# GRU gates by seven block products instead of eight, with partial sums forked in PSUM, in a four-layer graph network on one core

## The chip, the cores and the metric

The kernel runs on one core of a Trainium2 chip. The metric is device time in microseconds, as the median of the runs; the profile is of one further execution. PE is TensorE, PEld its weight load, DVE VectorE, ACT ScalarE, POOL GpSimd, SP the engine whose queue issues most of the DMAs. All matrices are float32.

## The reference

128 graphs of 128 nodes with 256 features go through four layers, each followed by a residual addition and a layernorm: `x = layernorm(x + layer(x, adj))`.

- Layer 0 is graph attention with 4 heads (scores, leaky relu, masked softmax, weighted sum, elu).
- Layer 1 is a gated graph network: three rounds of message passing, each with a GRU cell with shared gate weights.
- Layer 2 is a relational sum: one masked neighbour sum and one weight for each relation number in `adj`.
- Layer 3 is graph attention with one head.

The change is mostly about layer 1:

```python
for i in range(3):
    m = einsum("bnd,de->bne", h, weight[i])
    aggr = einsum("bst,bsd->btd", A, m)
    gi = aggr @ w_ih.T + b_ih            # i_r, i_z, i_n
    gh = h @ w_hh.T + b_hh               # h_r, h_z, h_n
    r = sigmoid(i_r + h_r)
    z = sigmoid(i_z + h_z)
    n = tanh(i_n + r * h_n)
    h = (1 - z) * n + z * h
```

## The kernel before, in words

**Tiles and stages.** The graphs are cut into 33 groups: 31 of four graphs, and a half group of two at each end. A tile of a full group has 128 partitions and 4 x 128 = 512 columns for each half of the features (`C = 2` halves). A group passes through `loads`, `head` (layer 0, L387), `body` (layer 1, L486) and `tail` (layers 2 and 3, L622). Each of these is a Python generator that records a few instructions at a time and yields.

**What sets the order.** Three strings of letters (`START`, `STEPS`, `END`, L42 to L61) say which generator takes the next step; a letter stands for a stage and a group relative to the current one (L43 to L54, L782 to L788). Each engine then runs its instructions in exactly the order in which they were recorded. In the middle, one pass through `STEPS` handles a head of a later group, the bodies of two groups and tails of earlier ones; such a pass is called a period here. Semaphores make an engine wait for another one's data or for a buffer to come free.

**Gates.** `fold` (L234) multiplies `weight[l]` into `w_ih` once, so that a round needs only the neighbour sum of h, called `agT`, and a folded weight `wc`. A gate (r, z, and the two parts of n, called nh and ni) is then a sum over h (`whh`) and `agT` (`wc`). For each output half c, `part` (L519) issues one matmul of 128 x 128 weights by 512 columns per input half and source into a bank of PSUM; `gate` has four banks and the other uses (`ps`) have four. So r and z take 8 matmuls a round each and nh and ni take 4 each. A float32 matmul of the program becomes two weight loads and two matmul instructions in the profile, so the profile's counts are twice the program's.

**The rest of a round.** ACT applies tanh to r and z (`sigmoid`, L535) and reads nh with its bias (L541); DVE combines r and nh (L543) and adds ni (L547); ACT takes tanh (L549); POOL forms h - n (L551); DVE finishes h (L557, L558). PE transposes h (L104), ACT copies it to SBUF (L509), PE multiplies by the adjacency, and DVE copies the result to `agT` (`neighbours`, L475 to L483).

**Other places.** `head` adds the attention score's row part, column part and mask in one DVE instruction per head and graph (L426), as `tail` does (L731); leaky relu and the row maximum follow on DVE (`softmax_unscaled`, L347 to L350), exp on ACT (L353). elu's minimum is on DVE (L332). Transposes that PE doesn't do go through DRAM: `to_dram` (L255) writes a tile, `from_dram` (L265) reads it back in four DMAs that permute 32 x 32 squares into one of four buffers `sq`, and DVE transposes inside the squares into another tile (L289, L391, L454, L648, L664, L751). `layernorm` (L293) writes its result to a new tile. All these DMAs are on SP's queue.

The instructions after the main part, which redo the work for relation numbers above 1, do not run with these inputs.

Of the kernel before, what the change touches and what calls it, by code (L numbers as in the profile page):

```python
# [16 lines left out]
P = 128  # L17
# [8 lines left out]
GATES, OTHERS = 4, 4  # L26
# [10 lines left out]
TERMS = {"r": {"h0", "h1", "a0", "a1"}, "z": {"h0", "h1", "a0", "a1"}, "nh": {"h0", "h1"}, "ni": {"a0", "a1"}}  # L37
# [3 lines left out]
FIRST = {"a": ("c", 0), "b": ("f", 0), "c": ("l", 0), "d": ("h", 0), "e": ("l", 1), "f": ("h", 1), "g": ("l", 2), "h": ("b", 0), "i": ("h", 2)}  # L41
START = """  # L42
abcbaaccabadbdaadddddddddaabeeacddadabbbbbbbbbbddbddbbdbbbbbbfbbbbbbbbdddddddddddgddddbbddddddfbbfdd  # L43
dddddffffdbfffffffdfddddfdgfhdfffehfbhhhfffffhhhhhhhhhhhhhfhhfhhhhhhfihhhhhhhfhhhhhhhhffhhhhhiffhhhh
hhhhhhfhhfhfhhhhhhhffffhihhhhhiffbiffhihffhbfiihfiihihhhihhh
"""
PERIOD = {"a": ("t", -2), "b": ("h", 0), "c": ("l", 2), "d": ("b", -1), "e": ("h", 1), "f": ("b", 0), "g": ("t", -3), "h": ("h", 2), "i": ("t", -1), "j": ("l", 1), "k": ("l", 0)}
STEPS = """
abbcaaaadadaeaddddddeabdddddeeeeafadbdfbegbcffddeeeeaaeeddddddfefaddfffaffffffffffffeffffffefhffiaff
aiiiefafffffaaffieiiafaifiiififaiaaaijfiifafaafafffiffiieffiiiikefffiaiifefaefffafiafefafffeefffehff  # L50
ffhfieeeeeefhhffhfhheieiehhfeefhh
"""
LAST = {"a": ("t", -3), "b": ("b", -2), "c": ("h", -1), "d": ("t", -4), "e": ("b", -1), "f": ("t", -2), "g": ("t", -1), "h": ("l", -1)}
END = """  # L54
aaaabbacbaacbbbcaabbbbbbbbbbdbccaabbbbabbbaeacebeeaafeeeeaeeefeeeeeeeeeeeeeeeeeeeefeaeeeeeeefafeffff
fffaaeaeefffafeaaaaafffffeeeffafefeefeeeeaaeffeeeeeeeeaeeeeeeeeeeeeeeeeeefefafeeefffeffeffeefeeeefgg
effffaeeeeeeefeeeeeeehffgggggggfagggggfggggggfgggfggffgfffggggfgfffggggggggagggfggfgggfgffgfgggggggg
ggggggggg
# [8 lines left out]
def kernel(ctx: ExitStack, tc: tile.TileContext, a: dict, out: bass.AP):  # L67
# [20 lines left out]
    def bank(*shape, tag="ps"):  # L88

        t = ring(pp, [P, 512], F32, tag, tag, GATES if tag == "gate" else OTHERS)  # L90
        n = 1
        for s in shape:
            n *= s
        if len(shape) == 1:
            return t[:, :n]
        names = "abcd"[: len(shape)]
        sizes = {k: s for k, s in zip(names[1:], shape[1:])}
        return t[:, :n].rearrange(f"p ({' '.join(names)}) -> p {' '.join(names)}", **sizes)
# [26 lines left out]
    def load_adj(st):  # L125
        st["adj"] = ring(sp, [P, st["n"], N], I32, "adj", f"adj_{st['g']}", 5)
        nc.sync.dma_start(st["adj"], adj[st["graphs"]].rearrange("g n m -> n g m"))

# [13 lines left out]
    def loads(st):  # L142
        for load in (load_x_squares, load_adj, load_rows, load_adj_squares):
            if st["g"] != 0 or load is load_adj_squares:
                load(st)
            yield

    def state(g):
        by_pe = {"head": g == 0, "tail": g == NG - 1}
        return {"g": g, "graphs": spans[g], "n": sizes[g], "relations": 1, "by_pe": by_pe}  # L150
# [10 lines left out]
    vec = ring(sp, [P, 4, D], F32, "y", "vec", 2)  # L161
# [5 lines left out]
    for l, tag in enumerate(("hr", "xb", "x3T")):  # L167
        w1.append(sp.tile([P, C, D], F32, tag=tag, name=f"w1_{l}"))
        nc.scalar.dma_start(w1[l], a["L1_gnn_weight"][l].rearrange("(c p) o -> p c o", p=P))
        if l == 0:  # L170
            for e, tag in enumerate(("wh3", "x2_0")):
                wih.append(sp.tile([P, 3 * D], F32, tag=tag, name=f"wih_{e}"))
                nc.scalar.dma_start(wih[e], a["L1_gnn_w_ih"][e * P : (e + 1) * P, :])
    whh = cp.tile([P, C, 3 * D], F32, tag="whh", name="whh")
    nc.scalar.dma_start(whh, a["L1_gnn_w_hh"].rearrange("(c p) o -> p c o", p=P))
# [23 lines left out]
    wc = cp.tile([P, L, C, 3 * D], F32, tag="wc", name="wc")  # L199
# [33 lines left out]

    def fold(st):  # L234


        for l in range(L):
# [8 lines left out]
            for c in range(C):  # L246
                for lo, hi in ((0, 512), (512, 3 * D)):
# [4 lines left out]
                    nc.vector.tensor_copy(wc[:, l, c, lo:hi], ps)  # L252
                    yield

# [10 lines left out]
    def from_dram(name, d):  # L265

        t = ring(sp, [P, d.shape[0]], F32, "sq", f"sq_{name}", 4)
# [3 lines left out]
    def turn_rows(st, x, tag, name, by_pe):  # L271

        n = x.shape[1]
        if by_pe:
            yield
            yield
            t = sp.tile([P, C, n * N], F32, tag=tag, name=name)
# [5 lines left out]
        else:  # L283
            d = to_dram(name, *(x[:, :, ts(c, P)] for c in range(C)))
            yield
            s = from_dram(name, d)
            yield
            t = sp.tile([P, C, n * N], F32, tag=tag, name=name)
            nc.vector.transpose(t.rearrange("p c m -> p (c m)"), s)  # L289
# [3 lines left out]
    def layernorm(y, st, name, bufs=1):  # L293
# [11 lines left out]
        def rest():  # L305
# [7 lines left out]
            o = st[name] = ring(sp, [P, n, D], F32, name, f"{name}_{g0}", bufs)  # L313
            for g in range(G):
                if g < n:
                    nc.scalar.activation(  # L316
                        o[:, g, :], y[:, g, :], AF.Identity, bias=mr[:, g : g + 1], scale=rs[:, g : g + 1]
# [6 lines left out]
    def residual_elu_norm(y, xin, st, name, layer, bufs=1):  # L324

        g0 = st["g"]
        half, rest = layernorm(y, st, name, bufs)
        ts_ = {}
        for k in range(0, G, 2):
            if k < st["n"]:  # L330
                t = ts_[k] = ring(sp, [P, 2, D], F32, "elu", f"elu_{layer}_{g0}_{k}", 2)
                nc.vector.tensor_scalar(t, y[:, k : k + 2], 0.0, None, ALU.min)  # L332
# [12 lines left out]
        yield from rest()  # L345

# [40 lines left out]
    def head(st):  # L387

        g0, n, adj_t, by_pe = st["g"], st["n"], st["adj"], st["by_pe"]["head"]
        xT = sp.tile([P, C, n * N], F32, tag="x0T", name=f"x0T_{g0}")  # L390
        nc.vector.transpose(xT.rearrange("p c m -> p (c m)"), st["x0s"].rearrange("p c m -> p (c m)"))  # L391
# [3 lines left out]
        if st["relations"] < R:  # L395
            above = sp.tile([P, n, N], F32, tag="adj_T", name=f"above_{g0}")
# [17 lines left out]
        for k in range(0, G, 2):  # L414
            if k >= n:
                for _ in range(8):
                    yield
                continue
            em = ring(sp, [P, 2, H, N], F32, "em", f"em0_{g0}_{k}", 2)
            for g in range(k, k + 2):  # L420
# [4 lines left out]
                for h in range(H):  # L425
                    nc.vector.scalar_tensor_tensor(  # L426
# [434 lines left out]
```

## Time and profile before

| what | value |
| --- | --- |
| median of 3 runs | 2969.25 us (2967.49 to 2970.28) |
| the profiled execution: device time | 2971.45 us |
| the profiled execution: span, first to last instruction | 2969.7 us |
| TensorE clock granted | 0.993 |
| busy: PE, DVE, ACT, POOL | 2898.6, 2026.4, 1326.1, 564.7 us |
| DMA | 254.93 MB, q1 busy 41.9% of 16 engines |
| one period of the middle, 1398.50 to 1488.85 us | 90.35 us |

How to read it: the lines that carry the prediction are quoted in it. The page gives the busy time of each engine, the chain of work that ended last (which engine and tile the end was waiting for at each moment, as shares of the span), and groups of equal instructions with count, busy time and mean length of one. The mean length of a matmul counts time that overlaps its neighbours, so the distance between starts in the timeline tells how long it occupies PE. In a timeline row, square brackets give the idle time of the engine just before, and what ended it. Busy shares are averages over the whole span.

### The profile page before, as it was taken

The numbers are of one execution on the slowest core, as the hardware profiler recorded it, in microseconds if no ns is written. First come the engines' busy times: TensorE is split into PE (matmuls) and PEld (weight loads), VectorE is DVE, ScalarE is ACT, GpSimd is POOL, SyncE is SP. The second block draws the span as 40 slices with busy tenths as digits, with TensorE's granted clock in tenths as the row PEclk, the third lists the DMA queues.
The fourth block names the chain that finished last, engine by engine and source line by source line (L and its number), as shares of the span: only waits on it lengthen the run. The fifth ranks groups of instructions, "written<-read, shape, count | busy, mean of one in ns | idle before, by whom it ended". The sixth has DMA issues, their size and how long they took to land.

```text
span 2969.7 us, 34231 instructions
## 1 busy us (share of the span) xinstructions
PE 2898.6 (98%) x10918; PEld 1691.9 (57%) x10918; DVE 2026.4 (68%) x4456; ACT 1326.1 (45%) x3310; POOL 564.7 (19%) x529
## 2 busy tenths in 40 slices
PE   7999999999999999999999999999999999999995
PEld 5655555555555555555555555555555555555564
DVE  5666767666767666767666677667676667676565
ACT  3444444444444444444444444444444444444343
POOL 0111222211222211222111222111222112222121
PEclk9999999999999999999999999999999999999997
DMA  4434444444445444445444444434444434444321
GB/s 112 80 79 80 89 86 92 85 98 84 85 82 100 85 96 84 80 84 102 88 89 83 88 82 97 95 77 91 93 82 93 97 78 89 86 88 84 75 54 42
DMA packets 1160922, 254.93 MB, mean 86 GB/s; under 512 B 931488, under 2 KB 1160224, under 8 KB 1160736
## 3 DMA queue, kind: packets, MB, share of 16 engines
q1 hardware_dynamic: 1157536, 248.87, 41.9%
q10 hardware_dynamic: 3200, 3.81, 0.5%
q8 instruction: 88, 1.44, 0.2%
q14 instruction: 98, 0.80, 0.1%
HBM read 144.97 MB, written 107.61 MB: 85 GB/s over the span
## 4 chain that ended last, share of the span: by engine, by line
PE 92%; DVE 4%; issue 1%; ACT 1%; DMA 1%; POOL 0%; DVEq 0%; SPq 0%; ACTq 0%; POOLq 0%
PE gate L101 63%; PE ps L101 27%; PE ps L104 2%; DVE d L557 2%; DVE aT L751 1%; ACT z L535 1%; PE psb L375 0%; DMA wih<-in_L_gnn_w_ih_dram 0%; DMA x<-in_x_dram 0%; ACT em L353 0%; DVE em L349 0%; DMA d_h0T<-x 0%; ACT x L316 0%; DVE st_x L303 0%; DMA vec<-in_L_gnn_a_src_dram 0%
## 5 line engine op out<-in xcount | busy, mean ns | idle before, releaser
L101 PE MATMUL gate<-agT,wc 128*128 128x512 f32 (+1 forms) x2376 | 1116.3, 583 | 3.3 <-DVE agT L483 3.3
L101 PEld LDWEIGHTS gate<-agT,wc 128*128 128x128 f32 x2376 | 444.1, 190 | 478.0 <-issue 459.4
L101 PE MATMUL gate<-h2T,whh 128*128 128x512 f32 (+1 forms) x792 | 375.9, 584 | 0.0
L101 PE MATMUL gate<-h1T,whh 128*128 128x512 f32 (+1 forms) x792 | 373.7, 581 | 0.0
L101 PE MATMUL gate<-h0T,whh 128*128 128x512 f32 (+1 forms) x792 | 362.5, 580 | 1.3 <-DVE h0T L289 1.3
L557 DVE SCALAR_TENSOR_TENSOR d<-z,d 128x512 f32<-128x512 f32 (+1 forms) x198 | 159.8, 807 | 270.9 <-ACT z L535 227.3
L543 DVE SCALAR_TENSOR_TENSOR n<-r,n 128x512 f32<-128x512 f32 (+1 forms) x198 | 132.9, 671 | 265.4 <-ACT n L541 265.3
L353 ACT ACTIVATE em<-em,nm 128x128 f32<-128x128 f32 x640 | 247.9, 391 | 52.9 <-DVE nm L350 52.9
L535 ACT ACTIVATE z<-gate,bhalf 128x512 f32<-128x512 f32 (+1 forms) x198 | 132.7, 670 | 257.0 <-PE gate L101 256.9
L316 ACT ACTIVATE x<-y,mr_x,rs_x 128x256 f32<-128x256 f32 x384 | 199.5, 591 | 100.2 <-DVE mr_x L311 100.2
L101 PEld LDWEIGHTS gate<-h0T,whh 128*128 128x128 f32 x792 | 145.4, 191 | 150.6 <-issue 149.3
L551 POOL TENSOR_TENSOR d<-h2T,n 128x512 f32<-128x512 f32 (+1 forms) x66 | 82.8, 1255 | 751.7 <-ACT n L549 751.7
L309 POOL TENSOR_TENSOR rs_x<-rs_x,neghalf 128x4 f32<-128x4 f32 (+1 forms) x99 | 108.4, 1095 | 612.3 <-DVE rs_x L308 612.2
L101 PEld LDWEIGHTS ps<-wh,aT 128*128 128x128 f32 x1280 | 171.5, 192 | 90.6 <-issue 49.2
L549 ACT ACTIVATE n<-n,bih 128x512 f32<-128x512 f32 (+1 forms) x198 | 139.6, 705 | 174.4 <-DVE n L547 172.9
L101 PEld LDWEIGHTS gate<-h2T,whh 128*128 128x128 f32 x792 | 146.0, 191 | 125.2 <-issue 113.4
L535 ACT ACTIVATE r<-gate,bhalf 128x512 f32<-128x512 f32 (+1 forms) x198 | 132.3, 668 | 190.2 <-PE gate L101 190.1
L101 PE MATMUL ps<-wh,aT 128*128 128x64 f32 (+1 forms) x1280 | 191.8, 297 | 17.9 <-DVE aT L751 13.5
L483 DVE COPY agT<-ps 128x512 f32<-128x512 f32 (+1 forms) x198 | 129.0, 652 | 113.2 <-PE ps L101 113.2
L101 PEld LDWEIGHTS gate<-h1T,whh 128*128 128x128 f32 x792 | 143.6, 191 | 109.9 <-issue 105.2
L541 ACT ACTIVATE n<-gate,bhn 128x512 f32<-128x512 f32 (+1 forms) x198 | 133.2, 673 | 146.7 <-PE gate L101 146.7
L551 POOL TENSOR_TENSOR d<-h0T,n 128x512 f32<-128x512 f32 (+1 forms) x66 | 82.1, 1244 | 528.0 <-ACT n L549 528.0
(116 smaller groups left out, 4030.7 us busy)
## 6 DMA issues: line engine op xcount, KB each, us to landing
d_em<-em SPq DMA_DIRECT2D x63, 512.0 KB, 3.4
sq_em<-d_em SPq DMA_DIRECT2D x252, 128.0 KB, 3.9
x0s<-in_x_dram SPq DMA_DIRECT2D x248, 64.0 KB, 2.7
x<-in_x_dram SPq DMA_DIRECT2D x31, 512.0 KB, 5.5
d_h0T<-x SPq DMA_DIRECT2D x62, 256.0 KB, 2.5
sq_h0T<-d_h0T SPq DMA_DIRECT2D x124, 128.0 KB, 3.2
d_h<-h3T SPq DMA_DIRECT2D x62, 256.0 KB, 2.4
sq_h<-d_h SPq DMA_DIRECT2D x124, 128.0 KB, 3.2
```

The lines of the kernel that those rows point to most:

```text
L101: nc.tensor.matmul(ps, lhsT, rhs, start=start, stop=stop)
L104: nc.tensor.transpose(ps, src, ident)
L309: nc.gpsimd.tensor_tensor(rs, rs, neghalf[:, :n], ALU.pow)
L316: nc.scalar.activation(o[:, g, :], y[:, g, :], AF.Identity, bias=mr[:, g : g + 1], scale=rs[:, g : g + 1])
L353: nc.scalar.activation(em[:, r, :], em[:, r, :], AF.Exp, bias=nm[:, i : i + 1], accum_out=den[:, i : i + 1])
L483: nc.vector.tensor_copy(into[c], ps.rearrange("p g n -> p (g n)"))
L535: nc.scalar.activation(t, gate[name][0], AF.Tanh, bias=bhalf[:, col : col + 1], scale=0.5)
L541: nc.scalar.activation(n, gate["nh"][0], AF.Identity, bias=bhn[:, c : c + 1], scale=0.5)
L543: nc.vector.scalar_tensor_tensor(n, tr, 1.0, n, ALU.add, ALU.mult)
L549: nc.scalar.activation(n, n, AF.Tanh, bias=bih[:, 2 * C + c : 2 * C + c + 1])
L551: nc.gpsimd.tensor_sub(d, hT[:, c, :], n)
L557: nc.vector.scalar_tensor_tensor(d, tz, 1.0, d, ALU.add, ALU.mult)
```

## The change

- **Gates.** The 2 x 2 block product (output halves by input halves, with the 512 columns cut into two halves of 256) is done by seven products of 128 x 128 by 256 columns in place of eight, in Winograd's form of Strassen's scheme. The left-hand sums of weights are formed once (`left_factors`); the right-hand sums of h and of `agT` are formed by POOL, four subtractions each per round and group (`right_sums`). A gate holds two PSUM banks, `sums` (output half 0) and `gate` (output half 1), two of each kind. Products 1 and 5 land in PSUM; ACT copies product 1 to the other bank and product 5 to SBUF; the later products accumulate on these copies; DVE adds product 5 to an intermediate sum twice.
- **Lanes.** `body` is replaced by four generators: `reset_and_new` (r, then ni), `new_and_update` (nh, then z), and one for each output half (`chunk_0`, `chunk_1`) with the elementwise steps. The three strings are new, and name these lanes.
- **Transposes in place.** The squares are loaded into the tile in which DVE then transposes them, source and destination the same; the buffers `sq` are gone. `layernorm` also writes over its input, and several tiles share or lose buffers. `adj` is loaded a second time for layer 3.
- **Moved between engines.** `agT` is copied by ACT (was DVE). The score is formed by an ACT addition of row and column part (`plus`, one per head and graph) and a POOL addition of the mask (was one DVE instruction). elu's minimum is on POOL (was DVE). Layer 2's bias is added by POOL to x2 in place, a little later.

The diff, cut to its core:

```diff
-GATES, OTHERS = 4, 4
+GATES, OTHERS = 2, 4
-TERMS = {"r": {"h0", "h1", "a0", "a1"}, "z": {"h0", "h1", "a0", "a1"}, "nh": {"h0", "h1"}, "ni": {"a0", "a1"}}
+TERMS = {"r": "ha", "z": "ha", "nh": "h", "ni": "a"}
...
+    def left_factors(l):
+        f = [factors[l][:, :, k] for k in range(S)]
+        nc.vector.tensor_add(f[4], f[6], f[3])
+        nc.vector.tensor_sub(f[5], f[4], f[0])
+        nc.vector.tensor_sub(f[2], f[1], f[5])
+        nc.vector.tensor_sub(f[6], f[0], f[6])
...
-        t = ring(sp, [P, d.shape[0]], F32, "sq", f"sq_{name}", 4)
         squares(t, d)
...
-            t = sp.tile([P, C, n * N], F32, tag=tag, name=name)
-            nc.vector.transpose(t.rearrange("p c m -> p (c m)"), s)
+            t = ring(sp, [P, C, n * N], F32, tag, name, bufs)
+            flat = from_dram(t.rearrange("p c m -> p (c m)"), d)
+            yield
+            nc.vector.transpose(flat, flat)
...
-                nc.vector.tensor_scalar(t, y[:, k : k + 2], 0.0, None, ALU.min)
+                nc.gpsimd.tensor_scalar(t, y[:, k : k + 2], 0.0, None, ALU.min)
...
+    def plus(e, row, col):
+        nc.scalar.activation(e, row, AF.Identity, bias=col)
...
-                    nc.vector.scalar_tensor_tensor(
-                        em[:, g - k, h, :], ps[:, h, :], wh[:, g, D + h : D + h + 1], nbias[:, g, :], ALU.add, ALU.add
-                    )
+                    plus(em[:, g - k, h, :], ps[:, h, :], wh[:, g, D + h : D + h + 1])
+                yield
+                e = em[:, g - k]
+                nc.gpsimd.tensor_add(e, e, nbias[:, g, :].unsqueeze(1).to_broadcast([P, H, N]))
...
+    def right_sums(t, B, c, name):
+        half = t.shape[1] // 2
+        lo, hi = t[:, :half], t[:, half:]
+        def minus(k, x, y):
+            B[k] = ring(sp, [P, half], F32, "T", f"T{k}_{name}", 12)
+            nc.gpsimd.tensor_sub(B[k], x, y)
+        if c == 0:
+            minus(5, hi, lo)
+        else:
+            minus(6, hi, B[5])
+            yield
+            minus(7, hi, B["12"])
+            minus(4, lo, B[6])
+        yield
...
-        nc.vector.tensor_copy(into[c], ps.rearrange("p g n -> p (g n)"))
+        nc.scalar.copy(t, ps.rearrange("p g n -> p (g n)"))
...
+    def gates(st, names):
+        cols = st["n"] * N
+        half = cols // 2
+        for l, layer in enumerate(st["layers"]):
+            for name in names:
+                first, second = bank(cols, tag="sums"), bank(cols, tag="gate")
+                layer["gates"][name] = first, second
+                c11, c12, c21, c22 = first[:, :half], first[:, half:], second[:, :half], second[:, half:]
+                def product(into, k, source, start=False, name=name, l=l, layer=layer):
+                    w = factors["h" if source == "h" else l]
+                    nc.tensor.matmul(
+                        into, w[:, SEL[name], k - 1], layer[source][k], start=start, stop=True, skip_group_check=True
+                    )
+                for i, source in enumerate(TERMS[name]):
+                    product(c21, 1, source, start=i == 0)
+                    yield
+                    product(c22, 5, source)
+                    yield
+                nc.scalar.copy(c11, c21)
+                p5 = ring(sp, [P, half], F32, "p5", f"p5_{name}{l}_{st['g']}", 3)
+                nc.scalar.copy(p5, c22)
+                yield
+                for source in TERMS[name]:
+                    product(c11, 2, source)
+                    yield
+                for source in TERMS[name]:
+                    product(c21, 6, source)
+                    yield
+                nc.vector.tensor_add(c12, c21, p5)
+                yield
+                for source in TERMS[name]:
+                    product(c12, 3, source)
+                yield
+                for source in TERMS[name]:
+                    product(c21, 7, source)
+                yield
+                nc.vector.tensor_add(c22, c21, p5)
+                yield
+                for source in TERMS[name]:
+                    product(c21, 4, source)
+                yield
```

## The prediction

> **What bounds the kernel now.** I read the page's busy times first, then its chain of work that ended last, then a stretch of the middle.
>
> ```profile
> span 2969.7 us, 34231 instructions
> PE 2898.6 (98%) x10918; PEld 1691.9 (57%) x10918; DVE 2026.4 (68%) x4456; ACT 1326.1 (45%) x3310; POOL 564.7 (19%) x529
> PE 92%; DVE 4%; issue 1%; ACT 1%; DMA 1%; POOL 0%; DVEq 0%; SPq 0%; ACTq 0%; POOLq 0%
> PE gate L101 63%; PE ps L101 27%; PE ps L104 2%; DVE d L557 2%; DVE aT L751 1%; ACT z L535 1%; PE psb L375 0%; DMA wih<-in_L_gnn_w_ih_dram 0%; DMA x<-in_x_dram 0%; ACT em L353 0%; DVE em L349 0%; DMA d_h0T<-x 0%; ACT x L316 0%; DVE st_x L303 0%; DMA vec<-in_L_gnn_a_src_dram 0%
> 1398.50:1488.85 90.35, 89.85 (x340) 51.98 (x340) 63.26 (x139) 41.45 (x103) 17.56 (x16) 1.00 0.43 88
> ```
>
> TensorE is the path: 92% of the chain, 63% in the gate products. The last line is one period of the middle (one group of four graphs): of 90.35 us TensorE is busy 89.85, VectorE 63, ScalarE 41, GpSimd 18. So a microsecond taken from TensorE counts in full while the others keep up.
>
> What a matmul occupies is read from starts in the timeline, not from its mean, because matmuls overlap (columns: start, length, form, count):
>
> ```profile
> 1477.00 1.95 PE L101 MATMUL ps<-rel,x 128*128 128x128 f32 x16
> 1478.79 1.88 PE L101 MATMUL gate<-agT,wc 128*128 128x512 f32 x4
> 1480.51 3.62 PE L101 MATMUL ps<-w,hr 128*128 128x256 f32 x16
> 1483.96 1.02 PE L101 MATMUL gate<-agT,wc 128*128 128x512 f32 x2
> ```
>
> 512 columns: (1480.51-1478.79)/4 = 0.430 us. 256 columns: (1483.96-1480.51)/16 = 0.216. 128 columns: (1478.79-1477.00)/16 = 0.112. A float32 matmul of the program is two such instructions. So the 256-column matmul, with a fresh weight each, already runs at half the price of the 512-column one; this matters below.
>
> The one place in the period where TensorE waits:
>
> ```profile
> 1465.11 2.49 POOL L651 TENSOR_TENSOR y<-y,x 128x512 f32<-128x512 f32 x2 [0.77 <-DVE y L648]
> 1466.51 1.64 DVE L557 SCALAR_TENSOR_TENSOR d<-z,d 128x512 f32<-128x512 f32 x1 [1.55 <-ACT z L535]
> 1468.18 0.69 DVE L558 SCALAR_TENSOR_TENSOR h1T<-d,n 128x512 f32<-128x512 f32 x1
> 1468.79 0.71 DVE L751 STREAM_TRANSPOSE aT<-sq_em 128x512 f32<-128x512 f32 x1
> 1469.55 1.13 PE L101 MATMUL ps<-wh,aT 128*128 128x256 f32 x4 [0.50 <-DVE aT L751]
> ```
>
> L557 takes 1.64 us in place of 0.69 while GpSimd adds at L651, everything behind it in VectorE's queue is late, and TensorE loses 0.50 us. The groups by form show the same block, in the 512-column row of L349, slower than the 1024-column one:
>
> ```profile
> L349 DVE SCALAR_TENSOR_TENSOR em<-em 128x1024 f32<-128x1024 f32 x64 | 77.8, 1216 | 0.0
> L349 DVE SCALAR_TENSOR_TENSOR em<-em 128x512 f32<-128x512 f32 x31 | 50.4, 1626 | 0.1
> L551 POOL TENSOR_TENSOR d<-h2T,n 128x512 f32<-128x512 f32 x62 | 80.0, 1290 | 718.9 <-ACT n L549 718.9
> L547 DVE TENSOR_TENSOR n<-n,gate 128x256 f32<-128x256 f32 x12 | 5.0, 416 | 2.1 <-PE gate L101 1.2
> ```
>
> **What the Trainium skill says.** "SBUF — State Buffer", section "Who interferes with whom": VectorE's second read port is GpSimd's, and one instruction holds it to its end; a VectorE instruction with two SBUF inputs collides, one with a PSUM input does not. The trace agrees (1.626 against 0.69 us above). "TensorE: Matmul & The Clock Gate", section "LDWEIGHTS": a weight load takes its columns over 1.2 GHz, 107 ns for 128; records here show 190 ns, and the 0.112 us spacing fits 107. "ScalarE: Activation LUTs", section "What ACT_TABLE_LOAD costs": an ACTIVATE with one pointer operand takes 280 + 0.833 N ns, about 93 of which overlap its neighbour; for N = 128 an estimate of 0.29 to 0.39 us; no row here is that exact form.
>
> **The change, part by part.**
>
> *Gate products.* There are 6 pairs (r, z from h and a; n from h; n from a) x 3 layers x 31 full groups = 558. Each goes from 4 matmuls of 512 columns to 7 of 256: 4 x 2 x 0.430 = 3.44 us becomes 7 x 2 x 0.216 = 3.02, less 0.42; over 558, -232 us (between -228 and -234 by the rounding). The 36 pairs of the two half groups: 4 x 2 x 0.216 against 7 x 2 x 0.112, 0.16 less each, -6. All on the path: -234 us taken together with the rounding, giving 2736.
>
> *VectorE.* Removed: the score adds (640, 140 + 36 us), the agT copies (129), elu's minimum (65). Added: two PSUM adds per gate, 744 of 256 columns at 0.416 (L547's row) = 310, and 14 for the half groups. Net -46: 1980 us, 72% of 2736.
>
> *ScalarE.* Added: two forks per gate, 744 copies of 256 columns at 0.37 (copies of that width from PSUM: 363 to 374 ns) = 275; the score add, 640 at 0.29 to 0.39, taken 0.30 = 192; agT copies 186 x 0.58 = 108. 1326 becomes 1900, 69%.
>
> *GpSimd.* Added: right-hand sums, 744 of 256 columns at 0.77 (the L551 rows of that width: 724 to 824) = 571, 24 for half groups; score additions of 512 columns, 159 x 1.27 = 202; elu's minimum 128 x 0.8 (between 0.5 and 1.27) = 102. 565 becomes 1464, 54%.
>
> No engine but TensorE is full, so none of this is on the path by its sum. What is on the path is the handoffs.
>
> *New waits.* Each gate now has three of them, 12 gates a group: products 1 and 5, then ScalarE forks, then product 2; product 6, then a VectorE add, then products 3 and 7; product 7, another add, then product 4. TensorE runs in order, so a late fork or add stops everything behind it, the other gate, heads and tails included. I laid the changed program's TensorE order against the rows above: between producer and consumer stands, at the median, 1.02 us of other matmuls for a fork that needs 0.49 (0.37 + two signals of 0.06), and 0.86 us for an add that needs 0.53. So about half of the handoffs have under 0.5 us to spare, where the waits of before mostly had 1 to 5 us. One has less than nothing: with two gate banks in place of four, "ni" reuses r's bank, and its first product stands 0.43 us behind r's last, while ScalarE's read needs 0.80: 0.37 x 93 = +34 us.
>
> *The shared port.* Before, blocking costs VectorE 26 us (L557: 186 x 0.14), 29 (L349) and 16 (L332), 71 in all; L332 moves away, 55 remain. GpSimd's work grows 2.6-fold: 55 x 2.6 = 143 us. From above: some 1030 two-input VectorE instructions meet GpSimd busy 54% of the time, 0.45 us left: 250. Before, TensorE lost 0.5 of 2.3 us blocked per period. With under half the slack I take half of 143: +72; ends 0 and 250.
>
> *Squares transposed in place.* Same transposes, same sizes: nothing, bounds -10 to +10 (an in-place form isn't in the trace). The load into its own square now waits on SP for the square's last reader, and SP's later loads queue behind it; these readers are 20 us or more past in the written order at the median, which hides it; uncovered, it would be a 3 us landing per group, +90. Reloading adj: 33 DMAs, 8 MB on 255, DMA at 43%: nothing. In-place layernorm, later xb, other tags: same counts. The prologue gains 16 VectorE additions of 384 columns at about 0.55 and a four-part load: +8, from 0 to +15, uncovered because TensorE idles there already.
>
> *Sum against the profiled execution:* 2969.7 - 234 + 34 + 72 + 8 = 2850. Its device time is 2971.45, 1.75 more than the span; the median of the runs, 2969.25, is 2.2 below that. They cancel: 2850.
>
> **The rivals.** (1) *The handoffs stay covered*, as the period of before shows a written order can: 2736 + 34 = 2770. For it: medians above need. Against: FIFO queues at 70% and an unplanned port block. (2) *Port and queues jam*, gain mostly lost: the port would carry GpSimd's 1464 and about 730 of VectorE, 80% of 2736. With 200 of the 250 on TensorE: 2736 + 34 + 170 to 200 = 2940 to 2970; I take 2940. (3) *Slower*: the adds, in VectorE's queue behind blocked two-input work, expose time at each handoff. Place: the PSUM adds before products 3, 7 and 4, and the forks; 36 a group, 1116 in all. The gain is gone at 234/1116 = 0.21 us each; at 0.3 it is 335 - 234: 3070. For it: spare time of 0.33 us at the median add, and L557's block of 0.95. Against: one late handoff gives slack to the next. (4) *It does not do what it says*: the 256-column products run at 0.245 us or more, since each needs its weights in that time, and the 234 vanish: 3000 with the waits. The 0.216 row speaks against it.
>
> **How the numbers follow.** Forecast 0.55 (own range 2800 to 2915), (1) 0.15, (2) 0.15, (3) 0.12, (4) 0.03. A fifth of (2) ends within 0.2% of before, 6 us, about what a measurement of this kernel can tell from no change: same 0.03. Faster 0.55 + 0.15 + 0.12 = 0.82, slower 0.15. The range 2755 to 2970 leaves out (3), (4) and the low edge of (1).
>
> **What would show it.** Right: gate matmuls at 0.216, a period of 85 to 88 us with TensorE idle 3 to 6 us of it, idle put down to the sums and gate tiles; L557-like rows with means over 0.8. Gate intervals near 0.245 show (4); a period of 84 shows (1); VectorE idle before TensorE's waits would refute the port as cause. I am wrong if TensorE's largest waits are on DMA or ScalarE.

## The result, and the profile after

The changed kernel takes 3017.5 us (median of 4 runs, 3012.9 to 3022.3) against 2968.4 for the kernel before (4 runs, 2967.3 to 2970.3): 1.0165 times as long, interval [1.0147, 1.0183]. The forecast was 2850, with a range up to 2970.

The page of the kernel after; the lines answer to those shown of before (span, busy times, chain by engine, chain by line):

```profile
span 3016.8 us, 44962 instructions
PE 2802.2 (93%) x14486; PEld 2310.3 (77%) x14486; DVE 2186.4 (72%) x4298; ACT 1830.2 (61%) x4952; POOL 1658.1 (55%) x1610
PE 69%; DVE 12%; POOL 8%; ACT 5%; issue 4%; DMA 1%; SPq 1%; POOLq 0%; DVEq 0%; ACTq 0%
PE gate L586 36%; PE ps L115 16%; PE sums L586 16%; POOL x L741 3%; DVE d L658 2%; POOL d L653 2%; ACT r L638 2%; DVE mr_x L357 1%; DVE h1T L659 1%; POOL em L794 1%; DVE h3T L659 1%; ACT em L394 1%; PE ps L118 1%; ACT x L362 1%; DVE o L387 1%
```

TensorE's share of the chain has fallen from 92% to 69%; VectorE and GpSimd took most of the rest, though they are busy only 72% and 55% of the time. One period of the middle (view of busy times by stretch):

```profile
1406.70:1497.98 91.28, 86.48 (x443) 71.37 (x443) 67.52 (x131) 56.57 (x153) 51.76 (x49) 0.98 0.47 91
```

It lasts 91.28 us. TensorE is idle for 4.8 of them (0.5 before), and the granted clock, the third number from the end, is 0.98 in place of 1.00. The period of before is 89.70 us, from the start of one transposition of h (1398.55) to the next (1488.25); the stretch of 90.35 us in the table above is a little longer than a period. After, periods of 91.28 and 89.65 us alternate in most of the middle, where 85 to 88 was forecast; over 27 periods the mean is 90.70. So of the time that the kernel lost, these 27 periods hold some 27 us, and what lies outside them, the start and the end of the program, some 20. What TensorE waited for, from the view of the waits (total us, times, longest):

```profile
PEld L424 <- DVE split L420: 84.7, 33, 3.5
...
PEld gate L586 <- POOL T_a L550: 54.1, 90, 1.2
PEld gate L586 <- ACT r L638: 42.1, 67, 0.8
...
PEld gate L586 <- DVE gate L614: 34.2, 73, 0.6
```

The largest is one wait per period, at an instruction that the diff does not touch: the transposition (L424) of the attention scores that VectorE splits into three bf16 parts. Its place, from the timeline over all engines (start, length, idle time before it in brackets):

```profile
1464.94 1.27 POOL L794 TENSOR_TENSOR em<-em,nbias 128x512 f32<-128x512 f32 x1 [4.00 <-ACT em L394]
1466.30 1.78 POOL L653 TENSOR_TENSOR d<-h2T,n 128x512 f32<-128x512 f32 x1
...
1468.11 1.20 DVE L658 SCALAR_TENSOR_TENSOR d<-z,d 128x512 f32<-128x512 f32 x1 [0.45 <-POOL d L653]
...
1468.85 1.05 POOL L550 TENSOR_TENSOR T_h<-h0T,T_h 128x256 f32<-128x256 f32 x1
...
1469.35 1.10 DVE L659 SCALAR_TENSOR_TENSOR h3T<-d,n 128x512 f32<-128x512 f32 x1
...
1469.86 1.17 POOL L550 TENSOR_TENSOR T_a<-agT 128x256 f32<-128x256 f32 x1
1470.37 0.69 DVE L417 CAST split<-wh 128x16 bf16<-128x16 f32 x1
1471.00 0.72 POOL L550 TENSOR_TENSOR T_h<-h0T 128x256 f32<-128x256 f32 x1
1471.10 0.65 DVE L418 TENSOR_TENSOR rest<-wh,split 128x16 f32<-128x16 f32 x1
...
1471.68 0.72 POOL L550 TENSOR_TENSOR T_h<-h0T,T_h 128x256 f32<-128x256 f32 x1
1471.78 0.65 DVE L419 CAST split<-rest 128x16 bf16<-128x16 f32 x1
...
1472.69 0.24 PE L424 MATMUL psb<-identb,split 128*48 128x128 bf16 x1 [2.24 <-DVE split L420]
```

Read it from the bottom. TensorE waits 2.24 us for the split. The split is four instructions of 16 columns; three of them take 0.65 to 0.69 us (the fourth 0.18, with no sum beside it); each ends with a GpSimd right-hand sum (T). They stand in VectorE's queue behind d and h3T, which the sums have stretched as well (1.20 and 1.10 in place of 0.69), and d waited for GpSimd's subtraction, behind GpSimd's new mask sum.

TensorE's waits can be added up without the modelled ends of matmuls: the distance from each matmul's start to the next, less the undisturbed spacing (0.430, 0.216 or 0.112 us for 512, 256 or 128 columns), summed over the span. Before: 112.6 us. After: 385.2. So the matmuls themselves gave back (2969.7 - 112.6) - (3016.8 - 385.2) = 225 us, and 273 were lost over that spacing: in waits, and in stretches at half the clock, which are found below. The experiments ask which part of the change these 273 belong to.

### The profile page after: what moved, and what is told of

It reads as the page before. It is cut to its first block, busy times and chain, and to the rows that moved or that the text cites. A ratio compares the mean times of both kernels' runs of the same rounds, so it can differ in the third digit from the quotient of the medians.

```text
span 3016.8 us, 44962 instructions
## 1 busy us (share of the span) xinstructions
PE 2802.2 (93%) x14486; PEld 2310.3 (77%) x14486; DVE 2186.4 (72%) x4298; ACT 1830.2 (61%) x4952; POOL 1658.1 (55%) x1610
## 4 chain that ended last, share of the span: by engine, by line
PE 69%; DVE 12%; POOL 8%; ACT 5%; issue 4%; DMA 1%; SPq 1%; POOLq 0%; DVEq 0%; ACTq 0%
PE gate L586 36%; PE ps L115 16%; PE sums L586 16%; POOL x L741 3%; DVE d L658 2%; POOL d L653 2%; ACT r L638 2%; DVE mr_x L357 1%; DVE h1T L659 1%; POOL em L794 1%; DVE h3T L659 1%; ACT em L394 1%; PE ps L118 1%; ACT x L362 1%; DVE o L387 1%
## 5 line engine op out<-in xcount | busy, mean ns | idle before, releaser
L586 PE MATMUL gate<-T_a,factors 128*128 128x256 f32 (+1 forms) x2376 | 708.2, 385 | 21.8 <-POOL T_a L550 21.6
L586 PE MATMUL gate<-T_h,factors_h 128*128 128x256 f32 (+1 forms) x2376 | 701.9, 382 | 10.1 <-DVE gate L614 3.8
L586 PEld LDWEIGHTS gate<-T_a,factors 128*128 128x128 f32 x2376 | 433.7, 192 | 110.9 <-POOL T_a L550 54.1
L586 PEld LDWEIGHTS gate<-T_h,factors_h 128*128 128x128 f32 x2376 | 441.0, 193 | 94.6 <-DVE gate L614 34.2
L586 PE MATMUL sums<-agT,factors 128*128 128x256 f32 (+1 forms) x1188 | 347.7, 384 | 0.6 <-ACT sums L596 0.4
L362 ACT ACTIVATE x<-x,mr_x,rs_x 128x256 f32<-128x256 f32 x384 | 199.6, 589 | 157.3 <-DVE mr_x L357 157.2
L586 PEld LDWEIGHTS sums<-agT,factors 128*128 128x128 f32 x1188 | 224.4, 194 | 40.2 <-DVE sums L606 8.6
L479 POOL TENSOR_TENSOR em<-em,nbias 128x512 f32<-128x512 f32 x128 | 179.8, 1415 | 39.3 <-ACT em L394 38.3
L394 ACT ACTIVATE em<-ps,wh 128x128 f32<-128x128 f32 x640 | 185.2, 387 | 20.9 <-PE ps L115 18.1
L586 PE MATMUL gate<-agT,factors 128*128 128x256 f32 (+1 forms) x594 | 180.4, 385 | 16.3 <-ACT r L638 12.9
```

The lines of the kernel that those rows point to most:

```text
L362: nc.scalar.activation(y[:, g, :], y[:, g, :], AF.Identity, bias=mr[:, g : g + 1], scale=rs[:, g : g + 1])
L394: nc.scalar.activation(e, row, AF.Identity, bias=col)
L479: nc.gpsimd.tensor_add(e, e, nbias[:, g, :].unsqueeze(1).to_broadcast([P, H, N]))
L586: nc.tensor.matmul(into, w[:, SEL[name], k - 1], layer[source][k], start=start, stop=True, skip_group_check=True)
```

## The experiments

Theory A: GpSimd's added work, in its queue and on the port that it shares with VectorE, makes releases late. Theory B: the handoffs within a gate (fork, two PSUM adds) cost by themselves, which was rival 3. Times are medians of 4 runs (of 20 for e10); the kernel before, measured alongside, took 2966.5 to 2968.3.

### The two suspects, alone and together

**e1.** The sums are left out:

```diff
-            nc.gpsimd.tensor_sub(B[k], x, y)
+            B[k] = x
```

> The right-hand sums are left out (products 4 to 7 read a block of h or agT itself), so GpSimd loses 798 subtractions, some 600 us; the 7 products, the forks and the two adds stay. Theory A (GpSimd's added work makes the releases late, by its own queue and by the shared port): TensorE's waits fall by more than half, 2840 to 2890 us. Theory B (the three handoffs per gate cost by themselves, about 0.2 us each): only the waits on the sums go, 2950 to 2980 us.

2858.8 us, 0.964 [0.9624, 0.9657] of before. The 798 subtractions cost 159 us. The rows of one split instruction, after and then without the sums (busy us, mean ns):

```profile
L417 DVE CAST split<-wh 128x16 bf16<-128x16 f32 x31 | 20.9, 673 | 0.0
```

```profile
L417 DVE CAST split<-wh 128x16 bf16<-128x16 f32 x31 | 5.2, 167 | 0.0
```

and TensorE's wait for the split without the sums, 84.7 us in the kernel after:

```profile
PEld L424 <- DVE split L420: 14.9, 31, 2.7
```

**e2.** The handoffs are left out:

```diff
-                nc.scalar.copy(c11, c21)
-                nc.scalar.copy(p5, c22)
...
-                    product(c11, 2, source)
+                    product(c11, 2, source, start=i == 0)
...
-                nc.vector.tensor_add(c12, c21, p5)
...
-                nc.vector.tensor_add(c22, c21, p5)
```

> The forks (two ScalarE copies a gate) and the two VectorE adds a gate are left out; the 7 products and the right-hand sums stay, so partial sums are not combined. Theory A: GpSimd is as busy as in the changed kernel, only some waits go, 2950 to 2990 us. Theory B: the handoffs were the loss, 2780 to 2840 us.

3016.5 us, no change. VectorE is busy 279 us less, and it gains nothing.

**e7.** Both edits together.

```diff
-            nc.gpsimd.tensor_sub(B[k], x, y)
+            B[k] = x
...
-                nc.vector.tensor_add(c12, c21, p5)
```

> Both the right-hand sums and the forks and adds are left out; the 7 products stay. With GpSimd relieved, do the handoffs cost anything? If they do: 2790 to 2825 us, well under the 2859 without the sums alone. If they are hidden: 2845 to 2860 us.

2828.3 us, 30.5 below e1: without the sums the handoffs do cost 30. Why they seemed free in e2 is seen in the clock. Granted clock by stretch in the kernel after, around the wait of 2.24 us, which ends at 1472.69 (the third number from the end):

```profile
1468.00:1472.60 4.60, 2.45 (x15) 1.88 (x13) 4.35 (x6) 2.00 (x9) 4.32 (x6) 1.00 0.29 88
1472.60:1474.60 2.00, 1.91 (x13) 1.27 (x13) 0.04 (x1) 1.26 (x4) 0.00 (x0) 0.92 0.64 131
1474.60:1476.00 1.40, 1.40 (x4) 1.17 (x4) 0.00 (x0) 1.40 (x7) 1.14 (x2) 0.50 1.00 157
1476.00:1478.00 2.00, 2.00 (x7) 1.60 (x6) 0.00 (x0) 2.00 (x8) 2.00 (x3) 0.58 1.14 153
1478.00:1480.00 2.00, 2.00 (x11) 1.69 (x10) 0.94 (x3) 0.36 (x2) 1.45 (x2) 1.00 0.52 70
```

From 1.6 us after the end of the wait TensorE runs at half its clock, for 3.4 us; in the middle of the span this happens in every second period. 256-column matmuls with a spacing of 0.38 to 0.46 us count it: 131 in the kernel after, 12 in e1, 272 in e2, where nearly every period has it. At 0.216 each, e2 loses 30 us more to the clock than the kernel after. Summed over all matmuls in the stretches that the trace's clock records give as half clock, the time over the undisturbed spacing is 71 us in e2, 36 in the kernel after and 9 in e1, which makes it 35. That is about what e2's missing handoffs gained: "no change" was two effects of nearly the same size, as far as these sums tell.

### What of the sums costs: their time, their reads, or the dependence

**e5.** The sums on VectorE.

```diff
-            nc.gpsimd.tensor_sub(B[k], x, y)
+            nc.vector.tensor_sub(B[k], x, y)
```

> The right-hand sums are formed by VectorE in place of GpSimd, all else as in the changed kernel. GpSimd loses some 600 us, VectorE gains 798 instructions at about 0.42 us, 320 us in all, and would stand near 2300 us of a span of 2900. Theory A (GpSimd's queue and port): most of what leaving the sums out gave comes back although the work is done, 2880 to 2930 us. If the dependence itself (h or agT, then four subtractions, then the product) made the loss, whoever does it: 3000 us or more.

3016.9 us, no change, with VectorE busy 2311 us: the sums are then late in VectorE's queue (products of T_a stand 106 us over the spacing, 64 in the kernel after).

**e9.** Each sum on 32 of its 256 columns.

```diff
-            nc.gpsimd.tensor_sub(B[k], x, y)
+            nc.gpsimd.tensor_sub(B[k][:, :32], x[:, :32], y[:, :32])
```

> Each right-hand subtraction is done on 32 of its 256 columns (the rest of its tile keeps zeros), by GpSimd, in the same place of its queue and with the same waits for h or agT and of TensorE for it. GpSimd loses some 400 us. If the time that GpSimd's sums take (its queue, the port) is the cause: 2870 to 2910 us, near the 2859 with no sums. If it is the dependence, an additional engine in the chain from h to the product: 2970 us or more.

2862.3 us, 3.5 above e1. The instructions, their places in the queue and what they wait for are all there, at 0.25 to 0.49 us each on average. So the dependence costs next to nothing; the time of each sum is the cost.

**e10.** GpSimd is kept busy as long, but reads nothing.

```diff
-            nc.gpsimd.tensor_sub(B[k], x, y)
+            for _ in range(3):
+                nc.gpsimd.memset(B[k], 0.5)
```

> Each subtraction is replaced by three memsets of the same tile, which take GpSimd about as long but read nothing: no dependence on h or agT, and no hold on the shared read port, but the place in GpSimd's queue stays filled. If the queue is the cause: 2980 to 3030 us. If the port and the dependence are: 2860 to 2900 us.

2964.1 us. The waits of TensorE in it:

```profile
PEld gate L587 <- POOL T_a L551: 106.1, 118, 1.8
...
PEld L424 <- DVE split L420: 14.9, 32, 3.5
```

The long wait at the split is gone (14.9 us, as in e1) although GpSimd is busier (1725 us against 1658), so GpSimd's load alone doesn't make it. Two of the split's rows in this run:

```profile
L417 DVE CAST split<-wh 128x16 bf16<-128x16 f32 x31 | 8.2, 263 | 0.0
...
L418 DVE TENSOR_TENSOR rest<-wh,split 128x16 f32<-128x16 f32 x31 | 5.4, 175 | 1.1
```

The subtraction with two inputs runs beside a memset as fast as alone (0.175 us, as in e1), while beside sums it took 0.63 on average: it needs GpSimd's reads to be held up. The cast is held up by a memset too (0.263 against 0.167), to the memset's end. So with sums of 0.72 us and more in place of memsets of 0.31 it is the port that stretches the split. The wait for T_a has doubled: GpSimd's queue alone makes products late. The two shares can't be read off this run, since the memsets take 692 us where the sums took 624 (GpSimd's busy time less that of e1), and wait for no data.

### Taking other work off GpSimd

**e3.** Score and mask in one VectorE instruction as before, elu's minimum on VectorE.

```diff
-                    plus(em[:, g - k, h, :], ps[:, h, :], wh[:, g, D + h : D + h + 1])
-                nc.gpsimd.tensor_add(e, e, nbias[:, g, :].unsqueeze(1).to_broadcast([P, H, N]))
+                    nc.vector.scalar_tensor_tensor(
+                        em[:, g - k, h, :], ps[:, h, :], wh[:, g, D + h : D + h + 1], nbias[:, g, :], ALU.add, ALU.add
+                    )
...
-                nc.gpsimd.tensor_scalar(t, y[:, k : k + 2], 0.0, None, ALU.min)
+                nc.vector.tensor_scalar(t, y[:, k : k + 2], 0.0, None, ALU.min)
```

> Of the changed kernel one part is undone: the score with its mask is again one VectorE instruction, and elu's minimum is on VectorE. GpSimd loses about 390 us, ScalarE 185, VectorE gains about 240. Theory A: 2900 to 2960 us, TensorE's wait for split (behind the score chain) mostly gone. Theory B: VectorE's queue delays the adds more, 3020 to 3080 us.

2989.4 us: 28 less. TensorE's wait at the split stays (74 us over the spacing, 80 after).

**e6.** Layer 2's bias added right after x2.

```diff
+        for g in range(n):
+            nc.gpsimd.tensor_add(y[:, g, :], x2[:, g, :], b2)
...
-                nc.gpsimd.tensor_add(x2[:, g, :], x2[:, g, :], b2)
...
-                nc.vector.tensor_add(y[:, s, :], ps, x2[:, s, :])
+                nc.vector.tensor_add(y[:, s, :], ps, y[:, s, :])
```

> Layer 2's bias is added by GpSimd as soon as x2 is there, as before the change, into layer 2's output tile, in place of after the relation products into x2 itself. Same instructions, same GpSimd time. If what matters is what stands ahead of the sums in GpSimd's queue (the chain shows 3.2 us of this add and 1.5 us of waiting before it in each period): 2900 to 2950 us. If it is GpSimd's total work or the port: 3000 to 3020 us.

3008.0 us: 9 less. The stall before the products of T_a shrinks by 28 us, and the one before the transposition of h grows by 43.

**e8.** As e6, with elu's minimum on VectorE.

```diff
-                nc.gpsimd.tensor_scalar(t, y[:, k : k + 2], 0.0, None, ALU.min)
+                nc.vector.tensor_scalar(t, y[:, k : k + 2], 0.0, None, ALU.min)
```

> The bias as early as before the change, and elu's minimum back on VectorE (128 instructions, GpSimd minus some 200 us, VectorE plus 55); all the work is done. If the queue ahead of the sums matters: 2870 to 2930 us; if only the port matters, 2970 to 3000 us.

3000.3 us.

**e11.** e3 and e6 together.

```diff
+            nc.gpsimd.tensor_add(y[:, g, :], x2[:, g, :], b2)
...
+                    nc.vector.scalar_tensor_tensor(
```

> All the work is done: bias early as in e6, score with mask and elu's minimum on VectorE as in e3. If what they took off adds up (28 and 9 us): 2975 to 2985 us. If the two remove different links of the same chain, and the chain is late only while one is left: 2930 to 2960 us.

3024.4 us (3022 to 3053), a miss: two edits that gain 28 and 9 alone lose 7 together. The half clock is part of it, 52 us here against 36 in the kernel after.

**e12.** As e8, with d = h - n on VectorE.

```diff
-            nc.gpsimd.tensor_sub(d, hT, n)
+            nc.vector.tensor_sub(d, hT, n)
```

> All the work is done: bias early, elu's minimum and h - n on VectorE; the score stays on ScalarE and GpSimd, the sums on GpSimd, which stands at some 1190 us. The chain at a round's end loses the hop to GpSimd and its blocked 1.8 us. If that chain is the cause of the waits: 2930 to 2965 us. If VectorE's load decides (2300 us): 2990 us or more.

3062.4 us, a miss: GpSimd has 479 us less to do than in the kernel after, and this one is 45 slower; against e8, its base, it is 62 slower. The transposition of h is 69 us over its spacing (35 after), but it was 76 in e8, so it isn't what was lost here: that is spread over gate products and others, 22 us of it at half clock. So GpSimd's load alone doesn't decide. Nor does VectorE's: it is busy 2252 us here, and 2250 in e18 below, the fastest complete kernel. What stands where in the queues is left.

**e4.** Eight products in the same lanes.

```diff
-                    product(c21, 1, source, start=i == 0)
...
+                    product(second, 1, 0, source, start=i == 0)
```

> The lanes, the written order, the in-place squares and the moved operations stay, but each gate is 4 matmuls of 512 columns per pair as before: no right-hand sums, no forks, no adds, and one of the left-hand sums left out so that the weight block is plain. TensorE gets its 232 us of matmul time back, with no new handoff. If the order and the moved parts cost nothing, 2960 to 2980 us as before; under A as under B close to that, since both causes are gone; if the order or the other moved parts cost, 3000 us or more.

3359.6 us, a miss that says nothing on the seven products: the order was written for other lengths, and four matmuls of 512 columns stand where products 1, 5, 2 and 6 did (490 us over the spacing). Nothing follows on what the new order costs by itself.

### The place: moving the split

After these, e2, e3, e6, e8, e11 and e12 still held 71 to 80 us at the split, and two theories stood. C: they come from that place alone, and can be had back by moving the split. D: the next late wait takes over.

**e13.** The split is recorded one step earlier, in the step of the copy that it reads.

```diff
                 nc.scalar.copy(wh[:, g, :], ps)
+            if g == n - 1:
+                full = split(wh[:, :, D + H :], f"0_{g0}")
             yield
```

> All the work is done; only an order changes. Head's four small VectorE instructions that split the column scores (L417 to L420) are recorded in the step of the copy they read, one step earlier: on VectorE they then stand ahead of the leaky relu and row maximum of a tail (L398, L399) and of d and h3T (L658, L659), which wait for GpSimd's mask sum and subtraction. Theory C: TensorE's 70 us at the transposition of the split (80 us over its nominal spacing, 10 before the change) come from these waits and from GpSimd's right-hand sums holding the port while the four small instructions run. Then nearly all 70 go: 2950 us, 2940 to 2965. Theory D: the next thing GpSimd makes late takes the place at once, and the time stays within 12 us of 3017.

3003.2 us: 14 less. The wait at the split is gone (80 us to 10.5), but products of h0T wait 35 us more and those of T 30 more. D seems right. But the split now also stands ahead of h0T's transposition (L335), and waits there for ScalarE's copy (82 us in 32 waits).

**e14** (with e3's edits), **e15** (with e8's), **e16** (with e1's):

```diff
+                full = split(wh[:, :, D + H :], f"0_{g0}")
```

> All the work is done. The earlier split, with score and mask in one VectorE instruction again and elu's minimum on VectorE, which by themselves gave 2989. Theory C: the two gains are at different places (the split still cost 74 us there), so they add: 2925 us, 2910 to 2945, below the kernel before. Theory D: 2980 or more.

> All the work is done. The earlier split, with layer 2's bias added right after x2 and elu's minimum on VectorE, which by themselves gave 3000. Theory C: 79 us were at the split there, so 2930 us, 2920 to 2950. Theory D: 2990 or more.

> Leaves out the right-hand sums, as the run without them did (2859). The earlier split on top. Theory C: with no sums to hold the port the split costs TensorE 11 us there in place of 80, so moving it gives 0 to 8 us: 2851 to 2859. If the split were late for the chain ahead of it alone, without the sums, it would give 70 here too: 2790.

2980.2, 2995.6 and 2901.6 us. e14 and e15 came out as theory D had them. But e16 is 43 above e1, outside both expectations: even with no sums the early place costs 43, most of it at gate products of h0T (41 us over the spacing against 7). So e13 had mixed a gain with a new loss.

**e17.** One letter of the written order is moved less far: behind h0T, the leaky relu and the maximum, but ahead of d and h3T.

```diff
 STEPS = """
-aabbacbbccdddefggg...
+gaabbacbbccdddefgg...
```

> All the work is done; one letter of the middle's written order is moved. The split of the column scores is recorded behind the transposition of h0T (L335), the leaky relu and the row maximum (L398, L399), but ahead of d and h3T (L658, L659). The earlier split that stood ahead of h0T too gave 3003: it took away the 70 us at the split, but 35 came up at the first product that reads h0T and 30 at products that wait for a sum. Theory C, repaired: h0T is no longer late, so about 35 of these return: 2970 us, 2955 to 2985. Theory D: the sums that follow on GpSimd are late anyway and take the place: 2995 or more.

2925.6 us: 92 below the kernel after, 0.9864 [0.9847, 0.988] of before. The same place in its timeline:

```profile
1331.92 1.78 POOL L653 TENSOR_TENSOR d<-h2T,n 128x512 f32<-128x512 f32 x1
...
1333.20 0.53 DVE L417 CAST split<-wh 128x16 bf16<-128x16 f32 x1
1333.65 0.74 POOL L550 TENSOR_TENSOR T_h<-h0T 128x256 f32<-128x256 f32 x1
1333.76 0.65 DVE L418 TENSOR_TENSOR rest<-wh,split 128x16 f32<-128x16 f32 x1
...
1334.66 0.59 DVE L420 TENSOR_TENSOR split<-rest,split 128x16 bf16<-128x16 f32 x1
...
1336.00 0.24 PE L424 MATMUL psb<-identb,split 128*48 128x128 bf16 x1
...
1336.48 0.70 PE L586 MATMUL gate<-T_a,factors 128*128 128x256 f32 x2 [0.24 <-POOL T_a L550]
```

Three of the split's instructions are still stretched by the port (0.53 to 0.65 us), but the first starts while GpSimd is still in d, and the last ends before TensorE comes. The matmul at L424 has no wait; the next one waits 0.24 us for its sum. The half clock is gone too: 13 matmuls with it, against 131. Theory C had 2970 and is 44 off: it gave back only the 35 us that h0T had lost in e13, and the products of sums gave back 37 more (the table below). The clock is not what it missed, since e13 had its full clock already (12 us at half clock; 9 here).

**e18.** The moved letter with e3's edits.

```diff
-aabbacbbccdddefggg...
+gaabbacbbccdddefgg...
...
+                    nc.vector.scalar_tensor_tensor(
```

> All the work is done. The moved letter, with score and mask in one VectorE instruction and elu's minimum on VectorE (2989 by themselves, 2980 with the split ahead of h0T). Theory C, repaired: 2945 us, 2930 to 2965, at or below the kernel before. Theory D: 2975 or more.

2900.3 us, 0.9775 [0.9759, 0.9792] of before, the fastest with all the work done, and 45 below where C had it. The changed kernel does end below the kernel before: by 1.4% with one letter of the order moved (e17), by 2.2% with score and minimum back on VectorE as well.

## Why the prediction was wrong, point by point

Where TensorE's time over the undisturbed spacing lies, in us by the tile that the matmul writes and reads (e1's products read h or agT where the others read a sum, so they count there; what matmuls lose at half clock is in their rows, 36 us of the 385 after and 9 of the 291 of e17):

| matmul | before | after | e1 | e13 | e17 |
| --- | --- | --- | --- | --- | --- |
| psb<-split | 10 | 80 | 11 | 11 | 11 |
| gate<-T_a and T_h | - | 107 | - | 137 | 100 |
| gate<-h and agT | 23 | 58 | 91 | 93 | 57 |
| sums<-h and agT | - | 40 | 25 | 25 | 25 |
| ps<-ident,h | 8 | 35 | 34 | 35 | 35 |
| all | 113 | 385 | 225 | 371 | 291 |

With the runs this makes an account, in the order in which the parts are added: before 2968; the products' spacing -225; waits that remain in e7, 196 - 113 = +83; handoffs, e1 less e7, +30; products that wait for a late sum, e17 less e1, +67 (the table agrees: 100 less the 34 by which e1's h and agT row is higher); the place of the split, after less e17, +92. Sum 3015, against 3017.5. Only the first two terms are measured apart from the times (they give 2826 for e7, which took 2828.3); the others are differences of runs. Against the forecast, 225 in place of 234 makes 9 us, the waits beyond the bank's 34 make 49, the handoffs 30, and the sums, 159 in place of 72, make 87. Less the forecast's 8 for the prologue, which the account doesn't list apart, these are the 167 by which it was too low.

- *Gate products, -234:* right. The spacing of 256 columns is 0.216 us with fresh weights, and 225 us came back. Rival 4 is out.
- *Bank return, +34:* plausible, not separated: gate products of agT are 34 us over their spacing (15 before), and the waits name ScalarE's r as the releaser 67 times. It is part of the 83. The rest of these was not forecast and not tried separately, so its cause stays open; in e7 the products that read relations are 26 us over (6 before), the transposition of h 17 (8 before), and gate products of h 26 (5 before).
- *The handoffs, "what is on the path":* 30 us. The forecast named them as what is on the path, but gave them no term beside the bank's; rival 3, which ended slower, put 335 there and was right in the sign alone.
- *"No engine but TensorE is full, so none of this is on the path by its sum":* failed. The 67 us are sums that come late from a GpSimd that is busy 55% of the time. It is a queue in order: at the start of a round, sums of h and agT, d, a mask sum and a bias stand in a row, and an average share says nothing on that row. The forecast priced GpSimd's work (1464 us; 1658 measured, of which some 180 is blocked time, where before had under 20) and laid none of it between two matmuls.
- *"The shared port ... I take half of 143 us: +72":* this is the step that failed most; the sums cost 159 us. The blocking itself was met by the upper bound of 250: VectorE's time above each group's undisturbed length (where it is exceeded by more than 40 ns) is some 250 us (some 75 before). What failed is the conversion into TensorE's loss by a share. TensorE's loss is not a share of the blocking: in e17 VectorE is blocked nearly as long (some 240), and the kernel is 92 us faster. It is what four short instructions at one place in the period decide. Two of the four are casts with one input, so they could not be among the "some 1030 two-input VectorE instructions"; yet the first cast went from 0.167 us without the sums to 0.673. The Trainium skill says this: "SBUF — State Buffer", section "Who interferes with whom", counts casts in the two-port mode among the instructions that take the pair, and the prediction used the two-input rule alone. (Its "1.626 against 0.69" sets two different instructions side by side; the block is seen in L557's 1.64 against the 0.69 it takes undisturbed.)
- *The clock:* not in the forecast at all. The wait of 2.24 us brings TensorE to half clock in every second period: 119 matmuls more than in e1, at 0.216 us each some 26 us, within the 92. The long periods are 1.6 us longer than the short ones, about half of 3.4. "TensorE: Matmul & The Clock Gate", section "HAM oscillation — how this bites in real kernels", warns of idle gaps over about 3.4 us; here 2.24 us was enough, so the measurement decides. The free-running window of 3.4 us that the page describes ("What's actually happening") agrees with the clock records of this trace: the 22 stretches at half clock in the kernel after all begin on one grid of 3.413 us, within 5 ns, and last one to three steps of it, but for the one that the end cuts off. In the middle they are 180.9 us apart, which is two periods and 53 steps. So the same wait falls differently on the grid from one period to the next, which fits that only every second one is hit; how much of a step must be idle isn't settled here.
- *Squares in place, nothing:* the waits of TensorE in the kernel after name a DMA once, `adj` at the start (14.9 us), and no load of squares. In e7 the loads of squares on SP (L134) hold 1% of the chain, so they aren't hidden wholly there; not tried by itself. *Prologue, +8:* not isolated; TensorE's first matmul starts 5.4 us later than before.
- *"I am wrong if TensorE's largest waits are on DMA or ScalarE":* they were on VectorE and GpSimd, and VectorE was blocked, not idle, ahead of them. The mechanism named was at work; its size at one place was missed. Of the rivals' mechanisms, the second, port and queues, was the nearest; it gave them 170 to 200 us and left the end below before.

Theory A stands in this form: the sums' time costs 159 us, 92 of them through one badly placed instruction group, and 67 as late sums. B is 30. D fell with e17. The 92 are nearly all wait and clock: the table has 69 less at the split, and the half clock costs 27 less. Open: what of the 67 another order would take away, whether e17's order gains anything without the sums (not tried, so that 92 and 67 divide the 159 is argued), the causes of the 49, and what the new lanes and the in-place tiles cost by themselves.

## What to carry to other kernels

In a kernel with a written order, don't convert an engine's busy or blocked time into a cost by a share. Go through the instructions for which the bounding engine waits, and ask for each what stands ahead of it in its own queue and in that of its releaser; a tiny instruction behind two blocked ones can cost more than hundreds of large ones. A change that loses may lose at a single place: before it is given up, its largest wait should be moved, and if a first move gains little, what the moved instruction now delays should be looked at.

## What the runs showed of the hardware that was not expected

- GpSimd is blocked as VectorE is: a sum of 256 columns takes 0.72 us alone and up to 1.25 beside VectorE. An instruction of 4 columns on VectorE (mr_x) went from 0.16 to as much as 1.23 us. A memset on GpSimd holds up VectorE's casts (0.167 to 0.263 us), and leaves its two-input subtractions alone (0.175).
- One wait of 2.24 us can halve TensorE's clock for 3.4 us, beginning 1.6 us after the wait. From matmul start to matmul start that gap is 2.62 us; in e10, whose largest gap in the middle of the span is 1.76, it doesn't happen (10 matmuls with the half clock's spacing in the whole span).
- The minimum with a constant on GpSimd takes 1.49 us for 512 columns, more than a sum of two tiles (1.27).
